# A transformer block on one core: other products once per head in one piece, values by head in DRAM, MLP steps of two chunks

## The chip, the cores and the metric

The kernel runs on one core of one Trainium2 chip. The metric is device time in microseconds for one execution. A core has a matrix engine (PE, with its weight loads listed as PEld), a vector engine (DVE), an activation engine (ACT), GpSimd (POOL), which here only issues DMAs, and SyncE (SP), which does the same. Each engine executes its own list of instructions in order; engines wait for each other by semaphores. PE writes to PSUM, eight banks of 2 KB per partition; ACT and DVE read PSUM and write SBUF. DMAs move data between DRAM and SBUF.

## The reference

A conditioned transformer block on x of 2 x 2048 x 576, float32, 16 heads of 36, MLP width 2304. Cut to what matters:

```python
ada = silu(c) @ W_ada + b_ada
shift_msa, scale_msa, gate_msa, shift_mlp, scale_mlp, gate_mlp = split(ada, 6, axis=-1)
h = layernorm(x) * (1 + scale_msa) + shift_msa
q, k, v = (h @ W_qkv + b_qkv)            # 16 heads of 36
attn = softmax((q * 36**-0.5) @ k.T)     # per head, 2048 x 2048
x = x + gate_msa * ((attn @ v) @ W_proj + b_proj)
h = layernorm(x) * (1 + scale_mlp) + shift_mlp
x = x + gate_mlp * (gelu_tanh(h @ W_fc1 + b_fc1) @ W_fc2 + b_fc2)
```

Everything stays in float32; the softmax subtracts each query's true maximum.

## The kernel before

**Front.** The conditioning, and LayerNorm, queries, keys and values of batch 0, are computed first (about 269 us). Queries and keys go to DRAM as `qk_d` (features by tokens), values as `v_d` (tokens by 16 heads x 37, column 0 of each head being 1, so that weighing also gives the softmax's sums).

**Units.** The main part has 8 blocks of 512 queries, each with 16 heads: 128 units. A unit's 2048 keys are taken in 4 slots of 512 keys. For a slot the kernel makes:

- *scores* (L658): 32 recorded matmuls of 64x64 tiles into two score tiles, called `s`, each of two PSUM banks;
- *keep* (L671): ACT copies both to SBUF, as `e`;
- *maxima* (L676): DVE takes running maxima into `acc`; after slot 3 it folds `acc` to 256 columns;
- *turn* and *across* (L694, L700): PE transposes `acc` (tile `mt`), DVE reduces it to `mx`; SP writes `mx` to DRAM as `m_d` and reads it back, broadcast to all partitions, as `m` (L709, L716);
- *less* and *exps* (L724, L728): DVE subtracts `m`, ACT takes the exponential;
- *weigh* (L744): PE multiplies by the values into `av`.

Scores run two units (8 slots) ahead of weighing. After slot 3, ACT copies `av` to `up` (one buffer), SP stores its lower half to `o_d` and `sum_d`, and POOL adds the upper half to them by accumulating DMAs (L764, L765).

**Other work.** The rest of PE's work is cut into steps that are put between a slot's scores and its weighing. They are the projections of batch 1 (`pq` for queries and keys, `pv` for values), and, for each block whose 16 heads are done, the attention's projection (`po`), the transposes of the normed rows (`pt`), the MLP's first product (`pf`) and second product (`py`). Products with 128 rows of contraction run as 128x128; the last 64 of 576 rows run as 64x64 tiles (`quads`, L106) after the transposes `mt` of the slot. A step yields its cost in PE microseconds, a function that takes its result out of PSUM, and perhaps its quads. `credit` gains RATE = 2.51 in each slot and pays for the steps; `fill` is called in slots 0 and 2, and in others if the credit allows. `pf` and `pq` come one 128-column chunk at a time. The light steps (`pt`) are done in slots 1 and 3.

PSUM has two score tiles (`ps_s`, 4 banks), two single banks (`ps_f`), which the steps use while units run, and `av` (2 banks).

**Beside it.** `gather(k)` is advanced once per slot: after a block's last head it loads sums and outputs, takes the sums' reciprocals, writes them to `rec_d`, loads them broadcast by heads as `r` (L1099) and multiplies (L1108). `tokens` does the LayerNorm of batch 1. `later` holds functions that `flush` calls near a slot's end: the second half of GELU, a unit's stores, a norm's first part.

**Order.** `tc.keep_in_program_order` keeps the order in which the Python code issues instructions on each engine. In the slot loop that order is:

```python
tiles = units[su].scores(sg); units[su].keep(sg, tiles)
dones = fill() if forced else []
units[lu].exps(lg)                      # the next slot's exponentials
if chain: subtract(G + 2); units[cu].turn()
for last in lasts: last()               # quads
units[u].weigh(g)                       # then across, maxima, subtract(G + 2)
flush()
for done in dones: done()
```

Values are loaded per unit in two parts of four slots' halves, part 0 by ACT's queue, part 1 by SP's, each as two DMAs in pieces of 37 floats.

Of the kernel before, what the change touches and what calls it, by code (L numbers as in the profile page):

```python
# [17 lines left out]
P = 128  # L18
# [4 lines left out]
def dit_block_kernel(  # L23
# [52 lines left out]
    v_d = [scratch.tile([L, H * HA], F32, name=f"v_d{b}") for b in range(B)]  # L76
# [84 lines left out]
    hp = ctx.enter_context(tc.tile_pool(name="h", bufs=2))  # L161

# [18 lines left out]
    with ExitStack() as front:  # L181
# [32 lines left out]
        def queries_keys_values(b, tb):  # L214
# [112 lines left out]
            for i in range(TB):  # L327
# [29 lines left out]
                seq(nc.sync.dma_start(out=v_d[b][ts(t, P), :], in_=vt.rearrange("p h e -> p (h e)")))  # L357
# [248 lines left out]
    with ExitStack() as main_part:  # L606
# [12 lines left out]
        class Unit:  # L619
# [12 lines left out]
            def load_values(self, part):  # L632

                t = np_.tile([P, NS * HA], F32, tag="v", name=f"v_{self.u}_{part}", bufs=3)
                self.vs.append(t)
                of = v_d[self.b].rearrange("(n p) e -> p n e", p=64)
                by = nc.scalar if part == 0 else nc.sync
                for r in range(2):
                    seq(
                        by.dma_start(  # L640
                            out=t[ts(r, 64), :].rearrange("p (n e) -> p n e", e=HA),
                            in_=of[:, ts(part, NS), ds(self.h * HA, HA)],
                        )
                    )
# [123 lines left out]
        state = {"wpr": None, "turn": 0, "slot": None, "norm": None}  # L768
# [6 lines left out]
        def room(name, n=2):  # L775

            if not state["busy"]:
                state["turn"] += 1
                if state["turn"] % 3:
                    t = ps_s.tile([P, 2, 512], F32, tag="s", name=name)  # L780
                    return [t[:, i, :] for i in range(2)]
            return [bank(f"{name}_{i}") for i in range(n)]
# [113 lines left out]
        def lit():  # L896

            while lights:
                cost, take = lights.pop(0)()
                yield cost if lights else 1.0, take  # L900
# [24 lines left out]
        def projections(b, tb):  # L925
# [15 lines left out]
            def values(i):  # L941
# [3 lines left out]
                def take():  # L945
# [4 lines left out]
                    for n in range(2):  # L950
# [5 lines left out]
                    seq(  # L956
                        nc.gpsimd.dma_start(
                            out=v_d[b][ts(tb * TB + i, P), :], in_=t[:, : H * HA]
                        )
                    )  # L960
# [10 lines left out]
            for at, (m, n) in enumerate(pairs):  # L971
                w = ws.pop(m)
                ev = mp.tile([P, 2, QB], F32, tag="gT", name=f"ev_{key}_{m}", bufs=5)
                pqs = []
                wc, wt = columns(w)
                tail = halves(hT, KC - 1)

                def rest(m=m, n=n, pqs=pqs, wt=wt):
                    if n == 2:
                        pqs.append(room(f"pq_{key}_{m}_1", 1)[0])  # L980
                        quads(pqs, wt, tail, (False, True))
                    else:
                        quads(
                            [pq[:, : QB // 2] for pq in pqs],
                            wt,
                            [tail[r][:, ts(r, QB // 2)] for r in range(2)],
                            (False, False),
                        )

                for j in range(n):  # L990
                    if j == 0:
                        pqs.append(room(f"pq_{key}_{m}_0", 1)[0])
                    if n == 1:
                        pqs.append(room(f"pq_{key}_{m}_1", 1)[0])
                    spans = [(j, slice(None), QB)] if n == 2 else [(r, ts(r, QB // 2), QB // 2) for r in range(2)]
                    for r, at_, n_ in spans:
                        for kc in range(KC - 1):
                            seq(
                                nc.tensor.matmul(  # L999
                                    pqs[r][:, :n_],  # L1000
                                    lhsT=wc[:, kc, ts(j, P)],
                                    rhs=hT[:, kc, at_],
                                    start=(kc == 0 and j == 0),
                                    stop=(kc == KC - 2 and j == 1),
                                )
# [471 lines left out]
```

## Time and profile before

| | |
|---|---|
| time, median of 3 runs | 3712.17 us (3706.52 to 3717.55) |
| profiled execution, its own time | 3718.53 us |
| its span, first to last instruction | 3716.8 us |
| granted TensorE clock, mean | 0.996 |
| PE busy | 3673.6 us |
| DVE busy | 2893.6 us |
| ACT busy | 2328.1 us |
| first scores / last weighing | 269.0 / 3478 us |
| DMA packets | 723011, of which 602310 under 512 B |

In the profile, a group's row gives the line, engine, operation, tile written and tiles read, shapes and count; then busy time and mean duration in ns; then the engine's idle time just before the group and what ended it. PE's recorded count is twice the number of float32 matmuls in the program (transposes count once). Durations of instructions that follow each other on one engine overlap by up to 0.1 us, so what an instruction costs its engine is read from start to start in the timeline. The chain of waits follows the work that ended last back to the start.

### The profile page before, as it was taken

Reading aid. Unit: us, or ns where it says so; the run is one execution under the profiler, and the core shown is the slowest. Engines: PE = TensorE matmul, PEld = TensorE weight load, DVE = VectorE, ACT = ScalarE, POOL = GpSimd, SP = SyncE. Lnnn points to the kernel's source line nnn. Section 1 sums busy time; section 2 is a strip of 40 time slices with the busy share of each in tenths; the row PEclk is TensorE's granted clock in tenths of the full one; section 3 lists DMA queues with packets and bytes.
Section 4 is the critical chain, followed back from the end, with each engine's and each line's share of the span. In section 5 each row is a group of like instructions: output and inputs, shape, how many; then the busy total and the mean of one; then the engine's idle time right before and its main releaser. Section 6 shows DMA issues by size and latency. Waiting matters only on the chain.

```text
span 3716.8 us, 91971 instructions
## 1 busy us (share of the span) xinstructions
PE 3673.6 (99%) x40054; PEld 2314.7 (62%) x40054; DVE 2893.6 (78%) x2872; ACT 2328.1 (63%) x2166; POOL 706.1 (19%) x1044
## 2 busy tenths in 40 slices
PE   8999999999999999999999999999999999999999
PEld 4556566655666656666666666665666665666565
DVE  4627888788888888888889888988878888888422
ACT  0006777667776677667667777777767766676321
POOL 0201121221113111312131212211131113111411
PEclk9999999999999999999999999999999999999999
DMA  7734454555445454636453545535363546444522
GB/s 246 266 109 113 105 115 107 117 122 110 81 106 123 89 99 88 133 73 110 91 132 78 121 73 127 109 84 96 87 132 74 111 88 119 87 107 68 139 71 70
DMA packets 723011, 406.28 MB, mean 109 GB/s; under 512 B 602310, under 2 KB 619736, under 8 KB 722608
## 3 DMA queue, kind: packets, MB, share of 16 engines
q0 software_dynamic: 77248, 205.28, 21.6%
q1 hardware_dynamic: 376816, 151.58, 18.5%
q10 hardware_dynamic: 268544, 43.53, 8.3%
q8 instruction: 315, 5.16, 0.7%
q14 instruction: 88, 0.72, 0.1%
HBM read 329.00 MB, written 71.21 MB: 108 GB/s over the span
## 4 chain that ended last, share of the span: by engine, by line
PE 91%; DMA 4%; DVE 2%; issue 1%; ACT 1%; POOL 1%; SPq 0%; DVEq 0%; POOLq 0%; ACTq 0%
PE av L744 23%; PE s L658 22%; PE py L1244 14%; PE pf L1196 13%; PE po L823 4%; PE pq L285 3%; PE pq_q L999 3%; PE pf L106 2%; PE pv L335 2%; PE pv_q L823 2%; DVE acc L676 1%; DMA x_b<-gp_d 1%; PE mt L694 1%; DMA rec_d<-sums 1%; DVE e L724 1%
## 5 line engine op out<-in xcount | busy, mean ns | idle before, releaser
L671 ACT COPY e<-s 128x1024 f32<-128x1024 f32 x1024 | 990.1, 1024 | 816.7 <-PE s L658 813.9
L724 DVE TENSOR_TENSOR e<-e,m 128x2048 f32<-128x2048 f32 x512 | 1165.0, 2281 | 46.8 <-DMA m<-m_d 46.5
L676 DVE TENSOR_TENSOR acc<-acc,e 128x1024 f32<-128x1024 f32 x768 | 939.4, 1223 | 195.8 <-ACT e L671 152.2
L728 ACT ACTIVATE e<-e 128x2048 f32<-128x2048 f32 x512 | 990.5, 1935 | 7.6 <-DVE e L724 6.7
L744 PE MATMUL av<-e,v 64*64 64x256 f32 (+1 forms) x16384 | 990.6, 380 | 1.5 <-ACT e L728 1.5
L658 PE MATMUL s<-qT,kT 36*64 36x256 f32 x16384 | 979.8, 376 | 2.6 <-PE pv L335 1.0
L744 PEld LDWEIGHTS av<-e,v 64*64 64x64 f32 (+1 forms) x16384 | 607.3, 132 | 336.0 <-issue 61.4
L658 PEld LDWEIGHTS s<-qT,kT 36*64 36x64 f32 x16384 | 625.8, 133 | 271.3 <-issue 6.6
L1244 PE MATMUL py<-w,gT 128*128 128x288 f32 x2304 | 581.8, 410 | 2.4 <-DVE x_b L1256 2.4
L1196 PE MATMUL pf<-h_b,w_b 128*128 128x512 f32 x1152 | 530.7, 604 | 0.0
L1244 PEld LDWEIGHTS py<-w,gT 128*128 128x128 f32 x2304 | 432.4, 190 | 147.2 <-issue 18.9
L764 POOL DMA_DIRECT2D o_d<-up x128 | 109.3, 854 | 2067.7 <-DMA o_d<-up 1245.9
L1196 PEld LDWEIGHTS pf<-h_b,w_b 128*128 128x128 f32 x1152 | 207.8, 189 | 266.9 <-issue 265.2
L1207 ACT ACTIVATE gT<-pf,bias 128x512 f32<-128x512 f32 x144 | 98.9, 687 | 187.7 <-PE pf L106 128.4
L700 DVE TENSOR_REDUCE mx<-mt 128x4 f32<-128x256 f32 x128 | 54.1, 423 | 172.6 <-PE mt L694 172.2
L676 DVE TENSOR_TENSOR acc<-e 128x1024 f32<-128x1024 f32 x128 | 155.6, 1216 | 4.5 <-ACT e L671 4.4
L1216 DVE SCALAR_TENSOR_TENSOR th<-th,gT 128x1024 f32<-128x1024 f32 x72 | 88.2, 1224 | 88.7 <-ACT th L1214 88.0
L676 DVE TENSOR_TENSOR acc<-acc 128x512 f32<-128x512 f32 (+1 forms) x256 | 142.9, 558 | 8.8
L1256 DVE TENSOR_TENSOR x_b<-py,x_b 128x288 f32<-128x288 f32 x192 | 81.5, 452 | 84.3 <-PE py L1244 84.2
L765 POOL DMA_DIRECT2D sum_d<-up x128 | 144.0, 1125 | 1.0 <-issue 1.0
L823 PE MATMUL po<-wpr_p,oT 128*128 128x288 f32 x512 | 132.6, 412 | 0.0
L285 PE MATMUL pq<-hT,w_in 128*128 128x512 f32 (+1 forms) x320 | 128.9, 554 | 0.0
(154 smaller groups left out, 2294.5 us busy)
## 6 DMA issues: line engine op xcount, KB each, us to landing
w<-w_d POOLq DMA_DIRECT2D x72, 576.0 KB, 6.0
v<-v_d ACTq DMA_DIRECT2D x256, 148.0 KB
v<-v_d SPq DMA_DIRECT2D x256, 148.0 KB
kT<-qk_d SPq DMA_DIRECT2D x256, 144.0 KB
w_b<-in_L_cond_W_fc_dram POOLq DMA_DIRECT2D x72, 512.0 KB, 5.2
qT<-qk_d SPq DMA_DIRECT2D x256, 72.0 KB
m<-m_d SPq DMA_DIRECT2D x256, 64.0 KB
w_d<-wg POOLq DMA_DIRECT2D x12, 864.0 KB, 6.8
```

Source lines behind the costliest of these rows:

```text
L285: nc.tensor.matmul(pq[:, r, :n], lhsT=w_in[:, kc, cols], rhs=hT[:, kc, at], start=(kc == 0 and not (two and r)), stop=(kc == KC - 2 and tw ...
L658: nc.tensor.matmul(s[ts(c, 64), i, ts(x, QH)], lhsT=self.kT[at, ts(2 * (2 * g + j) + x, 64)], rhs=self.qT[at, ts(c, QH)], start=True, stop ...
L671: seq(nc.scalar.copy(self.es[g][:, j], s))
L676: top = lambda out, x, y: seq(nc.vector.tensor_max(out, x, y))
L724: seq(nc.vector.tensor_sub(e, e, m))
L728: seq(nc.scalar.activation(e, e, AF.Exp))
L744: nc.tensor.matmul(self.av[ds(64 * i, wide), r, :QH], lhsT=self.vs[part][ts(r, 64), ds(t * HA, wide)], rhs=e[ts(r, 64), j, i, ts(x, QH)], ...
L765: seq(nc.gpsimd.dma_start(out=sums, in_=hi[0:1, :], accum_op=ALU.add))
L823: nc.tensor.matmul(outs[n][:, :C2], lhsT=src[:, kc, ts(i, P)], rhs=w_[:, kc, ts(n, C2)], start=(kc == 0), stop=False,)
L999: nc.tensor.matmul(pqs[r][:, :n_], lhsT=wc[:, kc, ts(j, P)], rhs=hT[:, kc, at_], start=(kc == 0 and j == 0), stop=(kc == KC - 2 and j == 1),)
L1196: nc.tensor.matmul(pfs[j], lhsT=wc[:, kc, ts(j, P)], rhs=h2[:, kc, :], start=(kc == 0 and j == 0), stop=(kc == KC - 2 and j == 1),)
L1244: nc.tensor.matmul(py[n][:, :C2], lhsT=gTs[f - f % 2][:, f % 2, ts(i, P)], rhs=w2s[f - f % 2][:, f % 2, ts(n, C2)], start=(j == 0), stop=( ...
```

## The change

1. **One visit per unit.** `fill` runs only in slot 0 (and in the 8 slots before the first weighing). It makes up to two heavy steps, the second if the credit is still positive. The transposes `mt` (`turn`) stand between them; the quads of both follow, then weighing. Up to two light steps come ahead of the heavy ones. `room` gives a slot-0 visit the two single banks first and then one score tile.
2. **Subtractions and exponentials.** In slot 0 the unit's three later slots are subtracted and exponentiated at once, ahead of `fill`'s results; the next unit's first slot is subtracted in slot 2 and exponentiated in slot 3.
3. **Steps of two chunks.** `pf` and `pq` yield once per pair of chunks (7.72), with both quads together. Their bias copies follow in one function, which also issues the load of the weights two steps on.
4. **GELU** is a queue: each flush does the second half of one and the first half of the next.
5. **Credit** starts at 0, gains 2.1 per slot up to slot 128, then 2.51.
6. **Values by head.** `v_d` is laid out as head, key within 64, 64-key group x 37. Storing a tile takes two DMAs of 37-float pieces, always on SP; loading takes two DMAs of 592 floats per partition, always on SP, in slots 1 and 3.

```diff
-    v_d = [scratch.tile([L, H * HA], F32, name=f"v_d{b}") for b in range(B)]
+    v_d = [scratch.tile([H, 64, L // 64 * HA], F32, name=f"v_d{b}") for b in range(B)]
...
+    def store_values(b, t, vt):
+        for r in range(2):
+            to = v_d[b][:, :, ds((2 * t + r) * HA, HA)].rearrange("h p e -> p h e")
+            seq(nc.sync.dma_start(out=to, in_=vt[ts(r, 64)].rearrange("p (h e) -> p h e", e=HA)))
...
-                of = v_d[self.b].rearrange("(n p) e -> p n e", p=64)
-                by = nc.scalar if part == 0 else nc.sync
                 for r in range(2):
                     seq(
-                        by.dma_start(
-                            out=t[ts(r, 64), :].rearrange("p (n e) -> p n e", e=HA),
-                            in_=of[:, ts(part, NS), ds(self.h * HA, HA)],
+                        nc.sync.dma_start(
+                            out=t[ts(r, 64), :], in_=v_d[self.b][self.h, :, ts(part, NS * HA)]
                         )
                     )
...
         def room(name, n=2):
-            if not state["busy"]:
+            free = state["banks"]
+            if state["busy"]:
+                if n == 1 and "h" in free:
+                    free.remove("h")
+                    return [state["half"]]
+                if free.count("f") >= n:
+                    for _ in range(n):
+                        free.remove("f")
+                    return [bank(f"{name}_{i}") for i in range(n)]
+                free.remove("s")
+            else:
...
+            t = ps_s.tile([P, 2, 512], F32, tag="s", name=name)
...
+        def gelu():
+            pending, state["gelu"] = state["gelu"], None
+            if pending:
+                pending()
+            if gelus:
+                state["gelu"] = gelus.pop(0)()
+
         def flush():
             for f in later:
                 f()
             later.clear()
+            gelu()
...
-                    yield (4.29, first, last) if j == 0 else (3.43, first)
+                yield 7.72, first, last
...
-        RATE = 2.51
+        RATE, EARLY, LATER = 2.51, 2.1, 2 * H * NG
...
-        credit = -32.0
+        credit = 0.0
...
-        def fill():
-            cost, dones = 0.0, []
-            while work and len(dones) < 2 and cost < 1.0:
...
+        def fill(most, between=lambda: None):
+            dones, heavy = [], 0
+            for _ in range(min(2, len(lights)) if most > 1 else 0):
+                cost, done = lights.pop(0)()
+                count(-cost)
+                done()
+            while heavy < most and (heavy == 0 or credit > 0):
...
+                count(-step[0])
+                if step[0] < 1.0:
+                    step[1]()
+                    continue
+                dones.append(step[1])
+                lasts.extend(step[2:])
+                heavy += 1
+                if heavy == 1:
+                    between()
+                if lights:
+                    break
+            if heavy == 0:
+                between()
             return dones
...
-            forced = g % 2 == 0 or G < 0 or credit > RATE
             tiles = units[su].scores(sg) if su < NU else None
             if tiles:
                 units[su].keep(sg, tiles)
-            if not forced:
-                for step in [lights.pop(0)() for _ in lights[:2]]:
-                    count(-step[0])
-                    step[1]()
-            dones = fill() if forced else []
-            if 0 <= G + 1 < NU * NG:
-                lu, lg = divmod(G + 1, NG)
-                units[lu].exps(lg)
-            if chain:
+            if g == 0 and here:
+                for n in range(1, NG):
+                    subtract(G + n)
+                    units[u].exps(n)
+            if tiles and not chain:
+                units[su].maxima(sg)
+            if g == 2:
                 subtract(G + 2)
-                units[cu].turn()
+            elif g == 3 and 0 <= G + 1 < NU * NG:
+                units[u + 1].exps(0)
+            dones = []
+            if g == 0 or G < 0:
+                whole = g == 0 and here
+                state["banks"] = ["f", "f"] + ["s"] * whole
+                dones = fill(2 if whole else 1, units[cu].turn if chain else lambda: None)
             for last in lasts:
                 last()
             lasts.clear()
-            if 0 <= G < NU * NG:
+            if here:
                 units[u].weigh(g)
             if chain:
                 units[cu].across()
                 if tiles:
                     units[su].maxima(sg)
...
             flush()
             for done in dones:
                 done()
```

## The prediction

> **What bounds the kernel now.** I read the page first: engine shares, granted clock, the chain that ended last, the costliest groups.
>
> ```profile
> PE 3673.6 (99%) x40054; PEld 2314.7 (62%) x40054; DVE 2893.6 (78%) x2872; ACT 2328.1 (63%) x2166; POOL 706.1 (19%) x1044
> ...
> PEclk9999999999999999999999999999999999999999
> ...
> PE 91%; DMA 4%; DVE 2%; issue 1%; ACT 1%; POOL 1%; SPq 0%; DVEq 0%; POOLq 0%; ACTq 0%
> ...
> L671 ACT COPY e<-s 128x1024 f32<-128x1024 f32 x1024 | 990.1, 1024 | 816.7 <-PE s L658 813.9
> L724 DVE TENSOR_TENSOR e<-e,m 128x2048 f32<-128x2048 f32 x512 | 1165.0, 2281 | 46.8 <-DMA m<-m_d 46.5
> L676 DVE TENSOR_TENSOR acc<-acc,e 128x1024 f32<-128x1024 f32 x768 | 939.4, 1223 | 195.8 <-ACT e L671 152.2
> L728 ACT ACTIVATE e<-e 128x2048 f32<-128x2048 f32 x512 | 990.5, 1935 | 7.6 <-DVE e L724 6.7
> L744 PE MATMUL av<-e,v 64*64 64x256 f32 (+1 forms) x16384 | 990.6, 380 | 1.5 <-ACT e L728 1.5
> L658 PE MATMUL s<-qT,kT 36*64 36x256 f32 x16384 | 979.8, 376 | 2.6 <-PE pv L335 1.0
> ```
>
> PE is busy 99% at full clock and is 91% of the chain; the rows of its two largest products show almost no idle time. So time can come only from how PE's busy time is spent, and be lost only where PE begins to wait. The timeline of PE shows the first, over one unit and in the tail (columns: start, duration, instructions merged):
>
> ```profile
> 1499.76 6.09 PE L1244 MATMUL py<-w,gT 128*128 128x288 f32 x24
> 1505.78 1.96 PE L744 MATMUL av<-e,v 64*64 64x256 f32 x32
> 1507.55 1.91 PE L658 MATMUL s<-qT,kT 36*64 36x256 f32 x32
> 1509.28 1.91 PE L744 MATMUL av<-e,v 64*64 64x256 f32 x32
> 1511.01 1.91 PE L658 MATMUL s<-qT,kT 36*64 36x256 f32 x32
> 1512.85 6.09 PE L1244 MATMUL py<-w,gT 128*128 128x288 f32 x24
> ...
> 3602.96 23.44 PE L1244 MATMUL py<-w,gT 128*128 128x288 f32 x96
> 3626.24 3.60 PE L1196 MATMUL pf<-h_b,w_b 128*128 128x512 f32 x8
> ```
>
> Read starts, not durations. Scores followed by weighing take 1.73 us, followed by py 1.84: entering 128-row work costs 0.11. Ninety-six py in a run take 23.28, so 24 are worth 5.82; here 6.02 pass: 0.20 more. Each visit to 128-row work between the 64x64 products thus costs 0.31 us. The transposes mt within a visit add nothing beyond their own 0.22.
>
> Where PE does wait, the timeline of all engines at a block's change shows why:
>
> ```profile
> 2713.19 0.42 DVE L700 TENSOR_REDUCE mx<-mt 128x4 f32<-128x256 f32 x1
> 2713.63 0.40 SPq L709 DMA_DIRECT2D m_d<-mx  x1
> 2719.48 1.20 SPq L716 DMA_DIRECT2D m<-m_d  x2
> 2727.64 2.29 DVE L724 TENSOR_TENSOR e<-e,m 128x2048 f32<-128x2048 f32 x1 [4.85 <-DMA m<-m_d]
> 2735.26 0.69 DVE L1108 TENSOR_TENSOR oT<-oT,r 128x512 f32<-128x512 f32 x1 [4.59 <-DMA r<-rec_d]
> 2735.56 0.59 ACT L756 COPY up<-av 128x512 f32<-128x512 f32 x1 [3.68 <-DMA sum_d<-up]
> 2741.95 0.68 PE L694 MATMUL mt<-ident,acc 128*128 128x128 f32 x2 [4.64 <-DVE acc L676]
> ```
>
> DVE is in order: a late load of m or r blocks the maxima behind it, then mt, then PE. Summing what each step of PE takes over its usual start to start, PE lost 36.9 us so between the first scores and the last weighing; 22.5 lie at three gathers (744, 2731, 3137 us).
>
> **The change, part by part.** Durations below are start to start of back-to-back instructions in the timelines: subtraction 2.20, maximum 1.14, folds 1.05, mx 0.34, GELU step on DVE 1.14, pair of additions 0.73; score copy 0.90, exponential 1.82, up 0.47, bias copy 0.70, modulation 0.67. A slot without a visit is 3.46 of PE, four are 13.84.
>
> 1. Fewer visits. In the order in which the instructions stand, PE's products are the same in number and form, before the last weighing and after it; visits within the units fall from 306 to 136 (128 units, 8 in the start). 170 x 0.31 = 52.7 us gained. Bounds: 0.20 (exit alone) gives 34; 0.36 (visits that end in 64-row remainders) gives 61. I take 0.31, the row of the commonest visit. [...]
>
> 2. Uneven units. PE's work per unit was about level (24.9 us per unit in the MLP blocks, by the stage windows). By the new order it runs from 15.7 (three transposes only) to 29.8 (two pf), 21 units under 21 us. DVE needs per unit 4 x 2.20 + 7 x 1.14 + 1.05 + 0.34 = 18.2 and a little, so it suffices, but its order now matters. Count from the unit's first scores. Its queue: three subtractions (6.60), mx, the first maximum, the additions, then maxima and the next unit's first subtraction. From the copies of slot 2 (7.9 us after the first weighing) come one maximum, subtraction, two maxima, folds: acc is ready about 2.7 us into the next unit, 3.9 with GELU. So mx ends at 9.7 and additions at 11.6. Against this, with the two score tiles given out in turn:
> - Single py, pf: the next scores need mx's tile at 10.7, 12.7. Covered; 0 to 0.5 for 11 py: 2 us. Single pv (3): at 9.3, 0.4 each: 1 us.
> - Two transposes, then py (12 units): py sits in a score tile, needed again at 10.6, free at 11.6: 1.0 each, 12 us. With pv (4): needed at 9.3, 2.3 each: 9. One transpose and pv (1): 2.8.
> - Transposes, then pf or pq in a score tile (9): exponentials end at 11.2, modulation and two bias copies at 13.2, needed at 12.2: 1.0 each, 9 us.
> - po po (6 after GELU): additions and statistics hold the tile 0.8 each: 5.
> - Three transposes only (2): the third's modulation stands behind three exponentials, 13.4 against 5.2: 8 each, 16.
> - Two steps otherwise, 12 to 16 us long: covered.
> Sum 57 us lost. Bounds: 28 if each is half hidden by later PE ends than I reckon; 110 with the round trip of rival A.
>
> 3. The old waits. The 14.4 us outside the gathers came from the old order; I take them as gone, what is late next being the list above. At gathers the reciprocal of the sums now stands in slot 2 of the unit. By rows, mx to the accumulation of the sums is 9.9 us (median), landing 3.4, the sums' load some 4: 27 us. Of seven gathers within the units, three start in units of 28 us (covered) and four in shorter ones. I take half of the 22.5: 11.3 gained. Bounds 22.5 and -15.
>
> 4. Values by head. Loads: 1024 packets become 64 per piece; the queue with half of them shows 268544 packets in 8.3% of 16 engines, 18 ns each. They leave ACT's queue, 256 issues x 0.60 = 154 us of an engine with slack on 63%; on SP they stand behind the reads of m. They were not what PE waited for: 0, cover being SP's idle and a unit of lead; bounds -10 (m's round trip shortened to its least) and +5. Stores go the other way, 2048 pieces of 148 B per tile. At 18 ns that is 2.4 us of 16 engines per tile; SP issues two of about 0.6 where one of 0.32 stood. In the front DVE waited 2.0 for the old store: 0, bounds 0 and +8. [...]
>
> 5. Queues. SP's stores of values wait for additions, before the next values' loads, needed a unit later: 0. On POOL the loads of MLP weights move behind the accumulations of up (mx + 10 us); landing about 28 us after the unit's start, needed at 31.8 once per block: 0, bound +3 x 7. up has one buffer, free 13.3 us after mx: at 23.0 in a 20.2 us unit. ACT then waits 2.8, the copies behind it, but the transposes need their tile only at 7.8; where py sits in it they wait 1.4 instead of the 1.0 charged: 0 taken, +5 as the bound.
>
> Sum: -52.7 - 14.4 - 11.3 + 57 = -21.4. The profiled execution took 3718.5 (span 3716.8 and 1.7 around it): 3697. The median of the runs is 6.4 lower: 3712.2 - 21.4 = 3691.
>
> **Rivals.** A, slower: the maxima's round trip. Loop: mx, m landed, subtraction, two maxima, folds, three subtractions, mx = 12.5 us plus the trip. Write to read of m is 4.4 median, 6.6 at nine in ten; read to landing about 4.2 to 8. At 8.6 the loop is 21.1; some 50 units are below 22.5. Once the trip exceeds 10 us the loop paces single units. At 1.2 us more in 50 and no gain at gathers: 3691 + 60 + 11 = 3762. For: 25 waits for m, up to 6.9 us. Against: double units between absorb it, and value loads collide less. B, no difference: gathers cost what they did and the trip adds 0.2 in 50 units: 3691 + 11 + 10 = 3712. C, better: waits half covered (28): 3662. That the change does not cut the visits is excluded by the order.
>
> **How the numbers follow.** Forecast (3672 to 3700) 0.36, C 0.12: faster 0.48. B 0.20. A (3724 and up) 0.32. About 0.3%, 11 us, is what can be told from no change. The range leaves one in ten either side: half of C below, the far part of A above: 3660 to 3752.
>
> **What would show it.** Right: about 136 visits, starts of 1.84 before each; PE waits before scores in units with transposes, with DVE adding or ACT modulating; some 8 us in the two units of transposes alone; no wait at double units. Wrong: DVE waiting for m in most single units (A), or PE waits summing far from 57 plus 11.

## The result, and the profile after

The changed kernel takes 4025.7 us (4021.9 to 4029.6), the kernel before beside it 3714.0 us: a ratio of 1.084 [1.082, 1.086], slower. The forecast was 3691 us, the top of its range 3752. These lines of the page of the changed kernel answer to those shown of before:

```profile
PE 3747.6 (93%) x40054; PEld 2398.4 (60%) x40054; DVE 2883.5 (72%) x2872; ACT 2370.5 (59%) x2166; POOL 696.1 (17%) x1028
...
PE 44%; DVE 17%; issue 7%; DMA 6%; ACT 4%; POOL 1%; SPq 1%; DVEq 0%; ACTq 0%; POOLq 0%
...
L674 ACT COPY e<-s 128x1024 f32<-128x1024 f32 x1024 | 990.5, 1019 | 463.7 <-PE s L661 421.7
L731 ACT ACTIVATE e<-e 128x2048 f32<-128x2048 f32 x512 | 977.9, 1913 | 452.0 <-DVE e L727 451.6
L727 DVE TENSOR_TENSOR e<-e,m 128x2048 f32<-128x2048 f32 x512 | 1148.2, 2283 | 17.0 <-DMA m<-m_d 17.0
L661 PE MATMUL s<-qT,kT 36*64 36x256 f32 x16384 | 1020.4, 385 | 104.5 <-ACT e L674 60.4
```

PE still has all its work, but is busy 93% instead of 99%; DVE holds 17% of the chain instead of 2%. The exponentials wait 452 us for subtractions (7.6 before), and the scores 104.5 us, most of it for ACT's copies. DVE itself waits 17.0 us for the maxima read back (46.8 before): their round trip, rival A, is not the cause.

Cut at the first scores and the last weighing, the spans compare so:

| us | before | after | more |
|---|---|---|---|
| to the first scores | 269.0 | 296.8 | 28 |
| first scores to last weighing | 3209.2 | 3464.3 | 255 |
| last weighing to the end | 238.6 | 265.2 | 27 |
| PE's waits in the middle part | 27.5 in 21 | 220.0 in 102 | 192 |

In the middle the visits did fall from 306 to 136, each starting 1.84 us after the work ahead of it, as forecast: 53 us. So some 308 us were lost there: 192 more of waits, and about 115 because PE worked at half rate after waits. PE's busy time in the middle part shows the second: it rose by 62 us, from 3181.7 to 3243.9, where 53 less were due. One unit shows both; PE first, then the windows over it (columns: us, busy time and instructions of PE, PEld, DVE, ACT, POOL, granted clock, DMA share, GB/s):

```profile
1373.80 0.82 PE L661 MATMUL s<-qT,kT 36*64 36x256 f32 x12
1376.39 1.15 PE L661 MATMUL s<-qT,kT 36*64 36x256 f32 x16 [1.76 <-DVE x_b L1147]
1377.27 3.62 PE L747 MATMUL av<-e,v 64*64 64x256 f32 x32
1380.65 1.97 PE L661 MATMUL s<-qT,kT 36*64 36x256 f32 x32
```
```profile
1376.00:1378.00 2.00, 1.61 (x24) 1.40 (x28) 1.97 (x5) 0.42 (x1) 0.00 (x0) 0.82 0.03 5
1378.00:1380.00 2.00, 2.00 (x24) 1.48 (x20) 1.52 (x2) 0.60 (x1) 0.00 (x0) 0.50 0.39 105
1380.00:1382.00 2.00, 2.00 (x37) 1.58 (x33) 0.00 (x0) 0.13 (x1) 1.61 (x2) 0.82 0.67 158
```

The additions after po make the scores wait 1.76 us; the next weighing takes 3.62 instead of 1.91, at a granted clock of 0.50. A wait of 1.8 us cost 3.5.

### The profile page after: what moved, and what is told of

Same layout as the page of the kernel before. It is cut to its first block, busy times and chain, and to the rows that moved or that the text cites. A ratio compares the mean times of both kernels' runs of the same rounds, so it can differ in the third digit from the quotient of the medians.

```text
span 4026.4 us, 92000 instructions
## 1 busy us (share of the span) xinstructions
PE 3747.6 (93%) x40054; PEld 2398.4 (60%) x40054; DVE 2883.5 (72%) x2872; ACT 2370.5 (59%) x2166; POOL 696.1 (17%) x1028
## 3 DMA queue, kind: packets, MB, share of 16 engines
q1 hardware_dynamic: 215792, 195.25, 22.5%
## 4 chain that ended last, share of the span: by engine, by line
PE 44%; DVE 17%; issue 7%; DMA 6%; ACT 4%; POOL 1%; SPq 1%; DVEq 0%; ACTq 0%; POOLq 0%
PE s L661 11%; PE av L747 10%; PE pf L1203 9%; PE py L1260 9%; DVE e L727 8%; DVE acc L679 7%; ACT e L674 2%; PE po L839 1%; PE pf L106 1%; DMA sum_d<-up 1%; DMA m_d<-mx 1%; DMA o_d<-up 1%; DVE gT L1237 1%; ACT xn_b L878 1%; DMA kT<-qk_d 1%
## 5 line engine op out<-in xcount | busy, mean ns | idle before, releaser
L731 ACT ACTIVATE e<-e 128x2048 f32<-128x2048 f32 x512 | 977.9, 1913 | 452.0 <-DVE e L727 451.6
L727 DVE TENSOR_TENSOR e<-e,m 128x2048 f32<-128x2048 f32 x512 | 1148.2, 2283 | 17.0 <-DMA m<-m_d 17.0
L661 PE MATMUL s<-qT,kT 36*64 36x256 f32 x16384 | 1020.4, 385 | 104.5 <-ACT e L674 60.4
L747 PE MATMUL av<-e,v 64*64 64x256 f32 (+1 forms) x16384 | 1005.9, 384 | 0.0
L661 PEld LDWEIGHTS s<-qT,kT 36*64 36x64 f32 x16384 | 643.6, 136 | 394.5 <-ACT e L674 78.0
L747 PEld LDWEIGHTS av<-e,v 64*64 64x64 f32 (+1 forms) x16384 | 639.2, 134 | 295.6 <-issue 48.3
L1260 PE MATMUL py<-w,gT 128*128 128x288 f32 x2304 | 591.3, 415 | 19.6 <-DVE gT L1237 11.1
L1203 PEld LDWEIGHTS pf<-h_b,w_b 128*128 128x128 f32 x1152 | 220.4, 196 | 294.5 <-issue 274.4
L1220 ACT ACTIVATE gT<-pf,bias 128x512 f32<-128x512 f32 x144 | 90.0, 681 | 230.5 <-PE pf L106 230.5
L993 PE MATMUL pq_q<-h_q,w_q 128*128 128x512 f32 (+1 forms) x240 | 108.2, 608 | 14.1 <-ACT h_q L156 6.7
```

Of the source, the lines that this page charges most:

```text
L661: nc.tensor.matmul(s[ts(c, 64), i, ts(x, QH)], lhsT=self.kT[at, ts(2 * (2 * g + j) + x, 64)], rhs=self.qT[at, ts(c, QH)], start=True, stop ...
L727: seq(nc.vector.tensor_sub(e, e, m))
L731: seq(nc.scalar.activation(e, e, AF.Exp))
L747: nc.tensor.matmul(self.av[ds(64 * i, wide), r, :QH], lhsT=self.vs[part][ts(r, 64), ds(t * HA, wide)], rhs=e[ts(r, 64), j, i, ts(x, QH)], ...
L1203: nc.tensor.matmul(pfs[j], lhsT=wc[:, kc, ts(j, P)], rhs=h2[:, kc, :], start=(kc == 0), stop=False,)
L1260: nc.tensor.matmul(py[n][:, :C2], lhsT=gTs[f - f % 2][:, f % 2, ts(i, P)], rhs=w2s[f - f % 2][:, f % 2, ts(n, C2)], start=(j == 0), stop=( ...
```

## Which units lose

An excess here is a unit's time from its first scores to the next unit's, less what its instructions take from start to start.

- Three transposes alone: 17.0 and 10.8 us (forecast 8).
- pv with transposes, in the early units: 6.9 to 10.4 (forecast 2.3). There ACT's copy to `up` waits for the accumulating DMA, and the copies behind it with it.
- Transposes, then pq or pf, nine units: 8 to 10 in the three of the early blocks, 3 to 5 in the six later ones, some 50 in all (forecast 1.0 each, 9 in all). In two of the three PE waits 6.7 us for ACT's modulation of the transposed rows, which stands behind the exponentials.
- po and then py: 9.0 to 9.3, six times (forecast 0). The timeline, engines mixed:

```profile
1408.93 0.16 DVE L147 SCALAR_TENSOR_TENSOR nm_b<-mv,rs_b 128x4 f32<-128x4 f32 x1
1409.13 4.46 ACT L878 ACTIVATE xn_b<-x_b,nm_b,rs_b 128x576 f32<-128x576 f32 x8 [4.09 <-DVE nm_b L147]
1413.50 1.90 ACT L674 COPY e<-s 128x1024 f32<-128x1024 f32 x2
1414.54 3.69 PE L661 MATMUL s<-qT,kT 36*64 36x256 f32 x32 [5.39 <-ACT e L674]
```

`both` now hands over the modulation of all four normed rows at once; 4.46 us of ACT stand ahead of the copies that the scores need.
- Two pf: 3.4 and, in the unit behind, 3.2 (forecast 0). GELU has one `th`: the second square waits 4.28 us, the copies behind it.
- po po 3.7 (0.8 forecast), transposes then py 1.1 (1.0), single py and pf 0 to 1.9 away from the gathers (0 to 0.5), two other steps in the MLP's units 0 away from the gathers (0).
- The seven gathers: some 20 us over two units at the first, 5 to 8 at each other, some 60 in all (forecast half of the 22.5 of before).

In front DVE waits for the values' stores, and in the tail PE waits for GELU: columns of the first line are engine, line and what it waited for, total, times, longest; the second fence is PE's timeline.

```profile
DVE vt L359 <- DMA v_d<-vt: 48.6, 5, 16.6
```
```profile
3812.24 1.24 PE L1260 MATMUL py<-w,gT 128*128 128x288 f32 x4 [2.39 <-DVE gT L1237]
3816.94 5.28 PE L1260 MATMUL py<-w,gT 128*128 128x288 f32 x12 [3.46 <-DVE gT L1237]
```

## The experiments

Ratios are to the kernel before on the same chip, with 95% intervals; waits are PE's between first scores and last weighing.

| run | median us | ratio | waits us |
|---|---|---|---|
| changed kernel | 4025.7 | 1.084 [1.082, 1.086] | 220 |
| e1 layout alone | 3729.8 | 1.008 [1.005, 1.010] | 20 |
| e2 change without the layout | 3976.5 | 1.075 [1.070, 1.079] | 199 |
| e3 stores early | 3948.8 | 1.067 [1.063, 1.071] | 173 |
| e4 transposes apart | 3979.6 | 1.075 [1.070, 1.081] | 181 |
| e5 GELU, rows, tail | 3920.5 | 1.059 [1.057, 1.060] | 188 |
| e6 all of these | 3859.2 | 1.042 [1.040, 1.045] | 144 |
| e7 pairs in before | 3834.8 | 1.036 [1.034, 1.038] | 112 |
| e9 pairs, slot 0 first | 3766.9 | 1.015 [1.013, 1.017] | 71 |
| e11 pairs, even units | 3769.8 | 1.016 [1.013, 1.018] | 75 |
| e15 GELU in slot 0 | 3813.2 | 1.028 [1.026, 1.030] | 95 |
| e10 e6, even subtractions | 3834.4 | 1.033 [1.031, 1.035] | 134 |
| e12 e6, short subtraction | 3668.6 | 0.989 [0.987, 0.991] | 21 |
| e13 before, short subtraction | 3690.5 | 0.994 [0.992, 0.996] | 10 |
| e14 changed, short subtraction | 3874.9 | 1.043 [1.041, 1.044] | 129 |
| e16 e6, one subtraction on POOL | 4239.4 | 1.145 [1.142, 1.147] | 387 |
| e17 before, the same | 4404.3 | 1.188 [1.184, 1.192] | 492 |

**Parts of the change.** e1 is the kernel before with the diff's lines on `v_d` alone, e2 the changed kernel without them. One of e1's lines:

```diff
-                seq(nc.sync.dma_start(out=v_d[b][ts(t, P), :], in_=vt.rearrange("p h e -> p (h e)")))
+                store_values(b, t, vt.rearrange("p h e -> p (h e)"))
```

> Kernel before with one part of the change alone: values by head in DRAM, their stores and loads on SP. Theory A (short waits of PE in the new order of the units lose the time, and the stores of 148-byte pieces lose it only in the front): the first scores start some 28 us later, at about 297 us instead of 269, the units and the tail stay as before, total about 3740 us. Theory B (the layout loses most of the time, because its small stores and the longer list on SP delay every other DMA): 3850 us or more, with waits for m, o_d or up spread over the units. If the smaller number of packets helps the units, they get shorter than 3209 us.

> Changed kernel with the values' layout and their queues as before. Theory A: the front's 28 us come back, and perhaps 10 to 30 us in the first 20 units, where value stores stand beside short units; the MLP blocks keep their waits: 3970 to 4000 us. Theory B: near the kernel before, 3700 to 3800 us.

Alone, the layout puts the first scores at 288.1 instead of 269.0 us; the middle part is 8 us shorter, which is within what runs of the kernel before differ by (3693 to 3722 us). Without it, the rest starts at 266.8 and still loses 7.5%. The layout is a minor part; its loss is seen in front alone, 16 to 28 us over the six profiles that have it. The waits of the front in e1:

```profile
DVE vt L359 <- DMA v_d<-vt: 32.9, 6, 12.4
```

e3 stores `up` right after the unit's last weighing, not a slot later; e4 takes the transposes out of slot 0:

```diff
+                units[u].store()
+
                 def store(done=units[u]):
-                    done.store()
```
```diff
-            for _ in range(min(2, len(lights)) if most > 1 else 0):
+            for _ in range(0):
...
+            if here and g % 2 and lights:
+                state["banks"] = ["f", "f"]
+                for cost, done in [lights.pop(0)() for _ in lights[:2]]:
```

> Changed kernel; a unit's stores of up are issued right after ACT has copied it, at the end of slot 3, ahead of the next unit's round trip of the maxima on SP. If ACT's wait for the single buffer up is what holds the score copies in units with transposes (7.5, 4.7, 8.7 us before pv), these waits fall to the 2 to 3 us that DVE's order gives and the time falls by 30 to 60 us. If the copies are late for another reason, it stays within 10 us of 4026.

> Changed kernel; the light steps (transposes of the normed rows) go to slots 1 and 3 as before, so that a heavy step gets the two single banks and not a score tile. Theory A: the waits before pv, pq, pf and py behind transposes go, and with them what they cost in clock: 80 to 130 us less, about 3900 to 3950. Theory C (one piece per unit is slow by itself, because three subtractions and three exponentials stand together): less than 30 us.

e3: pv with transposes falls from 9.5 to 3.8 and from 10.4 to 4.7: the late store, and with it `up`, was behind most of that. The first gather, too, falls from some 20 us to 1. e4: these units now lose 0.7 to 2.0 us, but some fifteen that lost nothing lose 2.5 to 3.5, and others rise, one from 4.7 to 9.0; scores that wait for copies rise from 60 to 95 us and for `mx` from 17 to 50. A wait taken from one unit came back in another.

e5 changes three places: a flush starts the next GELU half only where it finished none, the normed rows after po are modulated one per flush, and in the tail the gather and GELU go on faster. Cut to the main lines:

```diff
             if pending:
                 pending()
-            if gelus:
+            elif gelus:
...
-                later.append(f)
+                spread_rows.append(f)
...
+            gelu()
...
-            for _ in range(1 + state["slot"] % 2):
+            for _ in range(2 + state["slot"] % 2):
```

> The changed kernel (4026 us) with three places mended that the earlier runs left as they were: a flush starts the next GELU half only where none was finished (units with two pf lose 3.4 + 3.2 us over what their instructions take back to back, in six blocks), the four normed rows after po are modulated one per slot instead of in one slot (units with po then py lose 9.2 us, six times), and in the tail the gather advances twice as fast, so that py stand again between po and pt. Theory A (every PE wait costs itself and, from some 1.5 us on, half-rate work of some 3.5 us after it; places are independent): rows 9.2 to 3 each, 37 us; two pf 6.6 to 1 per block, 34 us; tail 265 to 245, 20 us; about 3935 us. Theory B (one piece per unit leaves no slack, so ACT's work comes too late somewhere else whatever is moved): the tail's 20 alone or a little more, 3985 to 4005 us, and new waits of scores in units that had none.

The rows give what was expected and more: po then py falls from 9.2 to 0.3 us, six times, 53 us. The tail is back at 238.8. GELU only moved. In the second unit of two pf, py now waits for it, with `mx` behind it on DVE:

```profile
1502.47 1.23 DVE L1244 SCALAR_TENSOR_TENSOR gT<-th,gT 128x1024 f32<-128x1024 f32 x1 [2.92 <-ACT th L1242]
1503.62 0.42 DVE L703 TENSOR_REDUCE mx<-mt 128x4 f32<-128x256 f32 x1
1503.76 7.05 PE L1267 MATMUL py<-w,gT 128*128 128x288 f32 x16 [5.78 <-DVE gT L1244]
```

e6 puts e2 to e5 together:

> All of it together on the changed kernel: values' old layout and queues, outputs stored right after a unit's last weighing, transposes pt in slots 1 and 3 behind scores and ahead of weighing, and the three mends of GELU, rows and tail. Visits in the main part are then 162 instead of 136 (before: 306). Theory A, the sum of what each gave alone (49 + 77 + 46) and 91 of the three mends: 4026 - 263 = 3763 us, PE's waits between first scores and last weighing at 60 us or under. If the waits fall to what before has (27.5), 144 fewer visits x 0.31 = 45 us stay as a gain: 3657 to 3670 us. Theory B (waits move): 3830 us or more, with waits of scores for ACT's copies still the largest group.

Front (267.4) and tail (238.9) are those of before; all that is left, 132 us, lies in the middle. By their ratios the single edits had given 36, 64, 33 and 94 us, together 227; put together they give 156. The sum was too simple. The time is theory B's (3830 us or more), but its sign is missing: the largest waits are not those for ACT's copies, 18.6 us, but those for `mx`, 84.8. What remains is named by the groups of PE, and by one unit that holds a single py, at a gather (DVE, then PE):

```profile
L663 PE MATMUL s<-qT,kT 36*64 36x256 f32 x16384 | 1014.9, 382 | 122.4 <-DVE mx L705 84.8 <-ACT e L676 18.6 <-DVE x_b L1156 9.3
```
```profile
1549.79 6.69 DVE L729 TENSOR_TENSOR e<-e,m 128x2048 f32<-128x2048 f32 x3
1559.40 1.23 DVE L1246 SCALAR_TENSOR_TENSOR gT<-th,gT 128x1024 f32<-128x1024 f32 x1 [2.92 <-ACT th L1244]
1560.55 0.42 DVE L705 TENSOR_REDUCE mx<-mt 128x4 f32<-128x256 f32 x1
1551.52 0.39 PE L699 MATMUL mt<-ident,acc 128*128 128x128 f32 x2
1561.02 1.98 PE L663 MATMUL s<-qT,kT 36*64 36x256 f32 x16 [6.35 <-DVE mx L705]
1562.78 3.50 PE L749 MATMUL av<-e,v 64*64 64x256 f32 x32
```

mt is done at 1552; `mx` reads it at 1560.6, behind three subtractions and a GELU half that waits for the exponentials of those subtractions. Its tile is the one the scores need.

**Is it the order, or DVE's time?** e10 is e6 with one subtraction and one exponential per slot, as before:

```diff
-            if g == 0 and here:
-                for n in range(1, NG):
-                    subtract(G + n)
-                    units[u].exps(n)
...
+            if 0 <= G + 1 < NU * NG:
+                lu, lg = divmod(G + 1, NG)
+                units[lu].exps(lg)
+            if chain:
+                subtract(G + 2)
```

> The run of all mends together (3859 us, PE waits 144 us, 85 of them scores that wait for DVE's reduction mx) with the change's second part undone as well: subtractions and exponentials one slot ahead in every slot, as before, so that one subtraction and not three stands ahead of mx on DVE. One visit per unit stays (162 visits). Theory A (the three subtractions make mx late): waits for mx fall to 20 us or under, and with the half-rate work behind them some 110 us go: 3740 to 3760 us. Theory B (one visit per unit is itself the loss: 13.84 us of unbroken scores and weighing outrun the copies, exponentials and maxima): 3820 us or more, with waits for mx or for ACT's copies as long as before.

Waits for `mx` fall from 84.8 to 4.8 us, as theory A has it, but mt now waits 82.2 us for `acc` and av 33.0 for exponentials; the ratio falls by one point only. Between these two orders it changes who is late, not that something is.

e12, e13 and e14 shorten the subtraction and leave every wait and the order; they take the maximum off one column in 256 only and so leave out part of the computation:

```diff
-                seq(nc.vector.tensor_sub(e, e, m))
+                seq(nc.vector.tensor_sub(e[:, :, 0:1], e[:, :, 0:1], m[:, :, 0:1]))
```

> The run of all mends together (3859 us, 162 visits, waits 144 us) with DVE's subtraction of the maximum done for one column of each 256 only, so that it takes some 0.1 us instead of 2.20 but still waits for m and is still waited for; it leaves out part of the computation (the maximum is taken off one query in 256). 512 x 2.1 us of DVE go. Theory C (in slots without other work DVE's 4.5 us per slot and ACT's 3.65 outlast PE's 3.46, and two score tiles give no lead): waits fall from 144 to 40 us or under, 3670 to 3720 us. Theory D (the waits come from the round trip of m and from the order of the queues): waits stay over 100 us, 3800 us or more.

> The kernel before with the subtraction for one column of 256 (it leaves out the same part). Theory C: before, slots 0 and 2 hold the other work and two slots together last 11 to 13 us, so DVE had time; only the waits at gathers and the few short units can go: 3680 to 3705 us where before takes 3702 to 3714. With this run the saving of visits can be read without waits: 144 fewer visits x 0.31 = 45 us between this run and the run of all mends with the same subtraction, if both have few waits.

> The changed kernel itself with the subtraction for one column of 256 (it leaves out the same part). Theory C: of its 220 us of waits those for DVE (x_b, mx, acc, and the copies of ACT that wait behind exponentials which wait for subtractions) go, those for the GELU queue, the norm's rows, the front and the tail stay (28 in front, 27 in the tail, some 60 in units with po then py, 30 in units with two pf): 3850 to 3900 us. Theory D: 3980 us or more.

The groups of e12:

```profile
L663 PE MATMUL s<-qT,kT 36*64 36x256 f32 x16384 | 988.9, 377 | 19.6 <-DVE mx L705 6.9 <-ACT h_b L156 4.2 <-ACT h_q L156 4.2
...
L729 DVE TENSOR_TENSOR e<-e,m 128x8 f32<-128x8 f32 x512 | 62.7, 167 | 101.7 <-DMA m<-m_d 101.5
```

With 1100 us off DVE, e6's waits fall from 144 to 21 us although DVE waits longer for m (101.5 us, 65.4 in e6), and the ratio falls from 1.042 to 0.989: under the kernel before, and 22 us under it with the same cut (e13). This is shown: what e6 lacks is DVE's time, not a shorter round trip. Whether that time is missed as a sum over the bare slots or as delay ahead of `mx`, e12 alone does not part; e10, where one subtraction stands ahead of `mx` and the waits come back elsewhere, speaks for the sum. Between e12 and e13 the middle parts differ by 21.2 us, e12 having 11.4 us more waits: 32.6 us for 144 visits, 0.23 each, or 0.30 with the some 10 us more that e12's granted clock loses (0.995 against 0.998). The saving was real. In the changed kernel (e14) the same cut takes the ratio from 1.084 to 1.043; beside e13, which has the cut too, 184 of the 312 us stay. The front (295.3), the tail (266.6), po then py (8.6 to 9.2 us) and, for the most part, the early units keep their losses. GELU does not: two pf and the unit behind fall from 3.4 and 3.2 us to 1.3 and 0.2, and po po from 3.7 to 0, so these were DVE's time as well.

**Fewer visits without one visit per unit.** e7 gives the kernel before the steps of two chunks, a step in slot 0 or 2 only with positive credit, and the tail of e5. e9 always fills slot 0, e11 fills slot 2 behind a short step and moves GELU's square one flush on, e15 moves both halves of GELU to slot 0:

```diff
-            forced = g % 2 == 0 or G < 0 or credit > RATE
+            forced = G < 0 or credit > (0.0 if g % 2 == 0 else RATE)            # e7
+            forced = G < 0 or g == 0 or (g == 2 and credit > 0)                 # e9
+            forced = G < 0 or g == 0 or (g == 2 and (state["first"] < 7.0 or credit > 4))  # e11, e15
...
             if chain:
                 subtract(G + 2)
+                gelu()                                                          # e15
                 units[cu].turn()
```

> The kernel before with only the steps of two chunks (pf, pq), one piece per slot as before, a step taken in slots 0 and 2 only while the credit is positive, credit from 0 and 2.1 per slot up to slot 128 as in the changed kernel, and a tail in which the gather advances one step more per turn. Visits in the main part 264 instead of 306: 42 x 0.31 = 13 us gained. Theory A: a unit's load is uneven only between 20 and 27 us, and DVE needs 18.2, so PE waits stay at some 30 us: 3690 to 3705 us on a chip where before takes 3702 to 3712. Theory B (a step of 7.7 us by itself brings waits, with their half-rate work): 3740 us or more, with waits in the units that hold one pf or pq.

> The kernel before with the steps of two chunks, as in the run of pairs alone (3835 us, visits 264, PE waits 112.3 us, of which 58.4 before mt in units whose slot 0 held no step), but slot 0 always takes a step and slot 2 only with positive credit; odd slots take none. Visits in the main part 231 instead of 306: 75 x 0.31 = 23 us gained. Theory A (the loss of that run is mt reaching PE too early in a slot 0 that holds nothing else, and the half-rate work after each such wait; the long steps by themselves cost 0 to 1.0 us in single units): 3680 to 3705 us where before takes 3701. Theory B (steps of 7.7 us lose by themselves): waits of mt are replaced by waits of scores, 3750 us or more.

> The run with pairs and slot 0 always filled (3767 us, profiled 3755; 231 visits; waits of av for exponentials 24.2 us in 33, of mt for acc 39.1 in 23, and the half-rate work behind the longer ones) with two edits: slot 2 takes a step whenever slot 0 held less than 7 us of steps, so that a unit holds two chunks alone or two shorter steps and is nowhere under 22.1 us except beside transposes; and GELU's square comes one flush after the bias copies, so that the next exponentials stand ahead of it on ACT. 230 visits. Theory A (waits come where a unit is too short for DVE's and ACT's 20 to 22 us of work, or where their work stands in the wrong order, not from long steps): waits fall to 35 us or under, as before, and the 76 visits saved show: 3690 to 3705 us beside 3714. Theory B (long steps cost waits by themselves): 3740 us or more.

> The run of even units (3770 us, 230 visits, waits 74.9 us, of which av for exponentials 33.9 in 51 units that hold one pf) with both halves of GELU in the next slot 0, ahead of mt, or where py needs them; the three bare slots of such a unit then hold 3.65 us of ACT each instead of 3.65 + 0.95. Theory C (ACT's pace in bare slots makes av wait): the waits of av go but for 5 us, and with them some 50 us of the units' 1.0 to 1.2 each: 3710 to 3725 us beside 3713. Theory D: the waits of av stay, or turn into waits of mt for acc of the same size, 3755 us or more.

All four are slower than before, and not by their long steps as such: in e7, e9 and e11 units of two py or two pf run without waits away from the gathers. In e7 the waits are of mt in units whose slot 0 is empty, where it follows the slot's scores at once:

```profile
1932.10 0.47 PE L694 MATMUL mt<-ident,acc 128*128 128x128 f32 x2 [2.73 <-ACT e L671]
1935.68 1.96 PE L658 MATMUL s<-qT,kT 36*64 36x256 f32 x32 [1.22 <-DVE mx L700]
```

e9 removes these and keeps 23 waits of mt for `acc` (39.1 us, the longest at gathers) and 33 of av for exponentials (24.2): a pf pair alone is followed by three slots of 3.46 us, in each of which ACT has 3.65 us of copies and exponentials, and twice 0.95 us of GELU. e11 did not lower them, and theory A's 3690 to 3705 us fell. e15 shows why they stay: its waits of av are 0.6 us instead of 33.9, so ACT's GELU was their cause, but GELU's DVE halves now stand ahead of `mx`, and the scores wait 51.1 us for that. This fits one reading: the pace of before, a short step in every second slot, leaves DVE and ACT their time, and each longer run of bare slots took it away.

**POOL for a quarter of the subtractions** (e16 on e6, e17 on before):

```diff
-                seq(nc.vector.tensor_sub(e, e, m))
+                seq((nc.gpsimd if g in (3,) else nc.vector).tensor_sub(e, e, m))
```

> The run of all mends together (3859 us) with the subtraction of each unit's last slot on POOL instead of DVE; nothing is left out. Of DVE's three subtractions ahead of mx two remain (4.4 instead of 6.6 us). Theory C (DVE's time in bare slots): waits fall from 144 to some 80 us, 3760 to 3800 us, if POOL takes no more than some 6 us for one and DVE is not slowed beside it. Against it stands that POOL also issues the accumulating DMAs and the loads of weights, and that no run has shown POOL at such work: if it takes 10 us or slows DVE, 3850 us or more.

> The kernel before with the subtraction of each unit's last slot on POOL; nothing is left out. Theory C: before has few waits to lose (27.5 us, and with all subtractions cut short 24 us were gained): 3700 to 3712 us beside 3714. If POOL is slow or DVE is slowed beside it: 3730 us or more.

Both lose far more than the bounds that were expected for a slow POOL (3850 us or more, 3730 or more). In e17 the exponentials wait 1040 us for POOL; the timeline shows one subtraction of POOL, what stood ahead of it in POOL's list, and DVE beside it:

```profile
1498.62 0.88 POOL L764 DMA_DIRECT2D o_d<-up  x1 [18.18 <-ACT e L728]
1500.33 5.13 POOL L724 TENSOR_TENSOR e<-e,m 128x2048 f32<-128x2048 f32 x1
1499.44 7.12 DVE L676 TENSOR_TENSOR acc<-acc,e 128x1024 f32<-128x1024 f32 x2 [2.41 <-ACT e L671]
```

Two maxima that take 2.55 us elsewhere take 7.12, 4.6 us more, while POOL needs 5.13. Order comes in as well: POOL had stood at the accumulating DMA for 18.18 us before it came to the subtraction. The two runs do not part these causes. No version run beat the kernel before with the whole computation in it.

**What a wait costs by itself.** e8, profiled once, appends 21 bursts of 20 matmuls to the kernel before, with chains of ACT copies between them:

> The kernel before with a stage behind its end that computes nothing of the result: 21 bursts of 20 matmuls 128x128 by 128x512 (some 17 us each), and between them a chain of 1 to 14 ACT copies, so that PE waits from about 0.7 to 7 us, each length twice. It measures what a wait costs beside itself. Theory A (from the units of the changed kernel): up to about 1.5 us the next burst starts at full rate; from 1.8 us on its first some 3.5 us of time run at half rate, so that it ends 1.7 to 1.9 us later, whatever the length of the wait. [...]

PE's timeline of part of that stage:

```profile
3773.73 17.43 PE L1442 MATMUL probe<-cx,wx 128*128 128x512 f32 x40 [2.09 <-ACT cx L1451]
3793.71 18.98 PE L1442 MATMUL probe<-cx,wx 128*128 128x512 f32 x40 [2.54 <-ACT cx L1451]
3815.68 17.43 PE L1442 MATMUL probe<-cx,wx 128*128 128x512 f32 x40 [2.99 <-ACT cx L1451]
3836.55 19.13 PE L1442 MATMUL probe<-cx,wx 128*128 128x512 f32 x40 [3.44 <-ACT cx L1451]
```

A full burst is 17.43 us. After waits of 0.7 to 2.1 us nothing is lost; after 2.54 us 1.5, after 2.99 nothing, after 3.44 1.7, after 3.9 to 6.6 us 2.2 to 2.7; the second round of each length gave the same within 0.1. Half rate after a wait is confirmed (granted clock 0.50 in the view below); a border at 1.8 us is not: the wait of 2.09 us cost nothing.

The record of the clock says more. In every trace of this case the granted clock changes only on one grid of 3.413 us. Cut on that grid, PE's view around the waits of 2.54 and 2.99 us reads (columns: us, busy time of PE, granted clock, DMA share, GB/s):

```profile
3790.03:3793.44 3.41, 1.14 (x3) 1.00 0.00 0
3793.44:3796.85 3.41, 3.14 (x4) 0.50 0.00 0
3810.51:3813.92 3.41, 2.18 (x6) 1.00 0.00 0
3813.92:3817.33 3.41, 1.65 (x4) 1.00 0.00 0
3817.33:3820.74 3.41, 3.41 (x9) 1.00 0.00 0
```

The shorter wait leaves PE busy for 33% of one window, and the next runs at half the clock; the longer one is split over two, 64 and 48% busy, and costs nothing. Over the 19 traces, from the first scores to the last weighing, all 361 windows at full clock in which PE was busy under 40% were followed by one at half; of 503 at 40 to 75% 136 were, of 16946 above none; what decides between 40 and 75% stays open. The second round of e8 came 215.19 us after the first, close to 63 windows (215.04), so it is no second sample of where a wait falls on the grid.

## Why the prediction was wrong, point by point

- **1, fewer visits:** right in count and start. At the 0.23 to 0.30 a visit of e12 against e13 the 170 are worth 39 to 51 us; 53 were taken.
- **2, uneven units, is the step that failed:** "so it suffices, but its order now matters. ... Sum 57 us lost", bounds 28 to 110. The middle part lost some 308 us, and PE's waits, expected at 57 plus 11, came to 220. The step took DVE's 18.2 us as an average over a unit and then followed each tile once, with every engine on time at the unit's start. It missed the rows handed over at once (55 us) and the GELU queue (some 40) altogether, gave early units with transposes and pv a quarter of what they lost, and units with transposes and pq or pf 9 us for 50. And it priced every wait at its own length: about 115 us lost to half-rate work behind the waits are in none of its terms, although the trace of before held an example (a wait of mt of 4.64 us, after which a weighing took 3.69 instead of 1.91). Of 33 waits of 2.25 us or more in the changed kernel 28 are followed by over 1 us of lost rate, of 45 under 1.25 us two.
- **3, the old waits:** DVE's waits for m did go, from 46.8 to 17.0 us, but the seven gathers cost some 60 us, the first 20 of them, where half of 22.5 had been taken.
- **4, values by head:** the loads as taken, 0 as far as e1 shows. The stores in front were taken as 0 with a bound of 8, which no run shows; they cost 16 to 28 (19 in e1, 28 in the changed kernel), and DVE waited 32.9 and 48.6 us for them.
- **5, queues:** `up` was taken as 0, bounded at 5. In the trace ACT's copy to `up` waits 32.4 us for the accumulation, and 36.6 more that the profile puts down to loads of keys and values; with the early stores of e3 both are gone, and the ratio gives 64 us.
- **The tail** was taken as unchanged since its contents are. Its order was not: GELU came a flush later and py no longer stood between po and the transposes, 27 us.
- **Rival A** (the round trip) had the right sign and the wrong mechanism: e12 is fast with longer waits for m. The range also ended at 3752, below this rival's own 3762, though it was given 0.32.

Of the 151 us that e14 takes out of the middle part 91 are waits, 220 to 129, and 60 are half-rate work behind them, by PE's busy time (3243.9 to 3183.9). What remains open: by e6 against e12, what a version of one visit per unit would need is less work on DVE, for which no run found a place.

## What to carry to other kernels

When PE is 99% busy and paced by a loop through other engines, even spacing of its other work is itself a resource: before bundling it, add up each engine's time in the stretch that is left bare (here three slots of 3.46 us for PE), not over the unit. An estimate from the changed kernel (over 1 us of lost rate after 28 of 33 waits of 2.25 us or more and after two of 45 under 1.25 us, in steps near 1.7): price a PE wait of the first kind at itself plus about 1.7 us, one of the second at itself. An experiment that shortens one engine's work but keeps all waits and the order tells "no time" from "late", which moving the work about did not.

## What the runs showed of the hardware

- Among the units the loss after a wait comes in steps near 1.7 us (in e8's bursts it was 1.5 to 2.7, or nothing): 1.7 behind the wait of 1.76 us in the first unit shown, 3.4 behind the one of 5.39 at po and py (6.88 us instead of 3.46 for scores and weighing). The granted clock is 0.50 there, in whole windows of 3.41 us: between the first scores and the last weighing of the changed kernel for one window 21 times, for two 19 times, for three 6 times. The length of the wait alone does not tell the loss: in e8 2.54 us cost 1.5 and 2.99 us nothing, with PE busy 33% of one window in the first case and 64 and 48% of two in the second; among the units 15 of 24 waits of 1.25 to 2.25 us cost over 1 us, in the bursts none up to 2.1.
- POOL and DVE hardly worked side by side on these operands: beside 5.13 us of POOL, DVE took 4.6 us more for two maxima. Over the whole of e17, with 670.4 us of subtractions on POOL, DVE's running maxima took 1141.4 us against 939.4 before, its 384 subtractions 2729 ns each against 2281, its 40 products with `r` 1937 ns each against 686: some 420 us more. The additions `x_b<-py,x_b`, with one input in PSUM, were not slowed (450 ns in e17, 452 before).
- Stores in pieces of 148 B held DVE up to 16.6 us at a time in the front, 48.6 us in all (L359); the stores of before held it 2.0 us, once, at the same line (L353).
